# Moving projections, an output projection and the next step's normalisation to other slots of a causal attention stage

## The chip, the cores and the metric

The program runs on one core of a Trainium2 chip. Its engines are TensorE (PE; its weight loads are listed apart as PEld), VectorE (DVE), ScalarE (ACT), GpSimd (POOL) and SyncE (SP), which here issues nearly all transfers. Each engine executes its own instructions in the order of the program and waits on semaphores for the others. The metric is the device time of one execution in microseconds; lower is better.

## The reference

A layer of causal attention with a pre-norm, and then a two-layer block of windowed attention with feed-forward. Only the first is touched here. With `x` of 4 x 1024 x 256 (four batch steps of 1024 tokens), 16 heads of 16 channels:

```python
def _layernorm(x, axis=-1, eps=1e-05): ...
def _L0_attn_ref(x, wq, bq, wk, bk, wv, bv, wo, bo):
    ...
    q = proj(wq, bq); k = proj(wk, bk); v = proj(wv, bv)
    scores = jnp.einsum('bhqd,bhkd->bhqk', q, k) * scale
    mask = jnp.triu(jnp.full((t, t), NEG, jnp.float32), k=1)
    attn = jax.nn.softmax(scores + mask, axis=-1)
    out = jnp.einsum('bhqk,bhkd->bhqd', attn, v)
    ...
    return out @ wo + bo
x = x + _L0_attn_ref(_layernorm(x, axis=-1), ...)
x = x + _L0_ffn_ref(_layernorm(x, axis=-1), ...)
```

All in float32. The normalisation has no gain or bias here; the second one, ahead of the feed-forward layers, is of the same form.

## The kernel before

The causal stage takes about the first 720 us; the two layers behind it take the rest, and nothing of them changes. The instructions of the causal stage stand in an order written out by hand: what is called first stands first on its engine.

**Chunks and slots.** The work is cut into 16 chunks `n` of four heads: chunk `n` belongs to batch step `b = n // 4`, and `c = n % 4` is its place in the step. Each chunk has 12 slots `u` (`NU = 12`). In a slot, `pair` (called twice, for two heads each) puts on PE the transposed scores `t` of chunk `n` (keys on partitions) and the scores `s` of chunk `n+1` (queries on partitions), both line 418. ACT makes the exponentials `et` from `t` (line 442), DVE takes the maxima of `s` (lines 430 and 436), which go into chunk `n+1`'s queries as an extra row so that its exponentials need no subtraction. So chunk `n+1` needs its `qbuf` and `kbuf` one chunk ahead of its own exponentials.

**Masks.** In slots 0 to 3 and 8 to 11 the block of keys crosses the diagonal. There POOL clears the part above the diagonal in `et` (`affine_select`, line 448), once for two heads, before the product with the values may read it. In slots 4 to 7 no mask is needed. The products `av` with the values (line 481) come two slots later (`LAG = 2`). A slot that holds a piece of side work for PE issues these products in one part, another slot in two parts of half the width.

**Banks.** The `t` scores have three PSUM banks, the `s` scores four; the side work's results (`pp`, `pv`, `pr`) use the banks of `s`. One product bank `av` is kept.

**Side work.** After the pairs of a slot come the functions that a plan holds for it (`plan[n][u]`, filled by `put`):

- `norm(b, t0, t1)`: DVE takes mean and variance of token tiles of step `b` (`bn_stats`, `bn_aggr`, lines 264 and 265), POOL the power -0.5 (line 161).
- `prep_x(b, t2)`: POOL normalises two token tiles into `xn` (line 275).
- `turn_x(b, g, i)`: DVE transposes two tiles in 32 x 32 blocks into `xturn` (line 298). Its second call for a group `g` of four tiles (`i = 1`) also issues 16 transfers of 32 KB from SP (line 308), which put the blocks in their places in `xnT`, the transposed, normalised input. There is one `xnT` buffer.
- `project(b, d, which, h)`: 16 matmuls (line 252) of `xnT` with `wq` (`which` = 0) or `wk` (1), for the channels of half `d` and the 256 tokens of quarter `h`; ACT adds the bias and writes the result to `dense` (line 365). There is one `dense` buffer each for q and k, so half `d+1` goes where half `d` was. Quarters 0 and 1 read group 0 of `xnT`, quarters 2 and 3 group 1.
- `spread(n, h)`: eight transfers from SP (line 377), which copy chunk `n`'s heads for 512 tokens out of `dense` into `qbuf` and `kbuf`.
- `put_maxima(n, half)`: DVE turns the maxima, SP sends them to DRAM (`way`, line 462) and, when these have landed, into the queries (line 465).
- `put_out`, `put_oT`: the products are divided by their sums and transposed; SP copies them to `oT` (four transfers, line 513).
- `out_b(b, t2)`: 32 matmuls (line 252, `pr`) with `wo` for two token tiles; ACT copies the result, POOL adds it to `x` (line 534). `out_s` takes the statistics for the next normalisation (DVE, then POOL's power); `out_c` normalises into `y_sb` on POOL (two instructions of line 557).

`quarters(n, b, d, first, *slots)` puts one projection in each of the slots named: q and k alternate, quarters ascend, starting from the place `first`. `outs(n, u, b, t2)` puts `out_b` in slot `u`, `out_s` one slot on, `out_c` three slots on. A slot number of 12 or more counts on into the next chunk.

**Where the touched work stands.** For a step `b`, the first chunk (`c == 0`: chunks 0, 4 and 8, and chunk 12, which has no step behind it) holds projections of half 1 of its own step and the statistics of step `b+1`; the second chunk (1, 5, 9) finishes the transposition of step `b+1` and projects its half 0; the third chunk goes on with that from its slot 0. In chunk 9, as an example, the plan before is: slot 0 `out_b(1,3)`, `spread(11,1)`, `turn_x(3,0,1)`; slot 1 `out_s(1,3)`, `prep_x(3,2)`; slot 2 `prep_x(3,3)`; slot 3 `out_c(1,3)`, `turn_x(3,1,0)`; slot 4 `turn_x(3,1,1)`; projections in slots 5, 6, 8 and 10, and in slot 0 of chunk 10 `project(3,0,0,2)`. `put_oT` of the chunk before stands in slot 3, `put_maxima` of the chunk behind in slots 4 and 11. Chunk 5 has two `scale_tab` on POOL besides (line 118).

Of the kernel before, what the change touches and what calls it, by code (L numbers as in the profile page):

```python
# [50 lines left out]
def kernel_body(  # L51
# [122 lines left out]
    with actx:  # L174
# [68 lines left out]
        NU = 12  # L243
# [322 lines left out]
        def put(n, u, fn, *a):  # L566

            plan[n + u // NU][u % NU].append((fn, a))

        def outs(n, u, b, t2):  # L570
            put(n, u, out_b, b, t2)
            put(n, u + 1, out_s, b, t2)
            put(n, u + 3, out_c, b, t2)

        def quarters(n, b, d, first, *slots):
            for i, u in enumerate(slots):
                put(n, u, project, b, d, (first + i) % 2, (first + i) // 2)

        for n in range(NCH):
            b, c = divmod(n, NC4)  # L580
            more = b + 1 < B
            if n >= 1:
                put(n, 2, put_out, n - 1, 1)
                put(n, 3, put_oT, n - 1, 1)
            if n + 1 < NCH:
                put(n, 4, put_maxima, n + 1, 0)
                put(n, 11, put_maxima, n + 1, 1)
            put(n, 6, put_out, n, 0)
            put(n, 7, put_oT, n, 0)
            if c == 0:  # L590
                if b:
                    quarters(n, b, 1, 3, 0, 2, 4, 6, 8)
                    outs(n, 7, b - 1, 2)
                    outs(n, NU, b - 1, 3)
                    put(n, 1, spread, n + 2, 0)
                    put(n, 3, spread, n + 3, 0)
                else:
                    quarters(n, b, 1, 2, 0, 1, 3, 4, 6, 8)
                    put(n, 2, spread, n + 2, 0)
                    put(n, 3, spread, n + 3, 0)  # L600
                put(n, 9, spread, n + 2, 1)
                put(n, NU, spread, n + 3, 1)
            if c == 0 and more:
                for i, u in enumerate((5, 7, 9, 10)):
                    put(n, u, norm, b + 1, 2 * i, 2 * i + 2)
                put(n, 8, prep_x, b + 1, 0)
                put(n, 10, turn_x, b + 1, 0, 0)
                put(n, 10, prep_x, b + 1, 1)
                n += 1
                put(n, 0, turn_x, b + 1, 0, 1)  # L610
                put(n, 1, prep_x, b + 1, 2)
                put(n, 2, prep_x, b + 1, 3)
                put(n, 3, turn_x, b + 1, 1, 0)
                put(n, 4, turn_x, b + 1, 1, 1)
                quarters(n, b + 1, 0, 0, 5, 6, 8, 10)
                n += 1
                quarters(n, b + 1, 0, 4, 0, 2, 3, 4)
                for i in range(2):
                    put(n, i, spread, n + 2 + i, 0)
                    put(n, 5 + 2 * i, spread, n + 2 + i, 1)  # L620
                for i in range(4):
                    put(n, (6, 8, 10, 13)[i], prep_b, b + 1, i)
                n += 1
                quarters(n, b + 1, 1, 0, 3, 5, 7)
                n -= 3
            if c == 3:
                outs(n, 9, b, 0)
                outs(n, 11, b, 1)
        n = -1
# [737 lines left out]
```

## Time and profile before

| | before |
|---|---|
| median of 3 runs | 1952.52 us (1952.07 to 1953.71) |
| the profiled execution | 1950.3 us |
| its span, first to last instruction | 1948.5 us |
| mean granted clock of PE | 0.973 |
| PE busy | 1883.4 us (97%) |
| DVE busy | 1345.5 us (69%) |
| ACT busy | 1006.4 us (52%) |
| POOL busy | 1029.3 us (53%) |
| `et<-t`, ACT line 442 | 327.8 us |
| `et<-et`, POOL line 448 | 102.5 us in 256 instructions, 407 ns each |

The chain of waits that ended last goes through PE for 86% of the span. A matmul's end is modelled, so a PE that is shown as busy may also be waiting: what a stage costs is read from the distances between its slots, by the first exponential (ACT, line 442) of each slot. The first exponential of a chunk starts at 55.0 us in chunk 0, 94.6 in chunk 1, 229.4 in chunk 4, 270.4 in chunk 5, 407.7 in chunk 8, 448.3 in chunk 9, 496.9 in chunk 10, 658.7 in chunk 14 and 694.1 in chunk 15.

Times in views are microseconds from the span's start. A row of a timeline has the start, the time taken, the engine and line, what is written from what, and how many instructions are merged; a row of a stretch has its length, then each engine's busy time in it, the granted clock and the share of the transfer engines.

### The profile page before, as it was taken

To read this page: it belongs to the slowest core of one execution; us is meant where nothing else is said; L and a number is where in the kernel's file an instruction comes from. 1 tells how busy PE (TensorE), PEld (TensorE's weight loads), DVE (VectorE), ACT (ScalarE), POOL (GpSimd) and SP (SyncE) were. 2 spreads that over 40 slices of the span, in tenths; PEclk is the share of its full clock that TensorE was granted. 3 is DMA by queue.
4 is the path that set the end of the run, shared out by engine and by line. 5 is a ranking of instruction groups with operands and counts; after the bars stand their busy time and mean duration, and the time that the engine had idled before them with its cause. 6 is when DMAs were issued, how large, how long until landed. Compare 5 with 4: busy or idle time off the path is not lost.

```text
span 1948.5 us, 51314 instructions
## 1 busy us (share of the span) xinstructions
PE 1883.4 (97%) x19258; PEld 1026.8 (53%) x19258; DVE 1345.5 (69%) x4092; ACT 1006.4 (52%) x2649; POOL 1029.3 (53%) x1268
## 2 busy tenths in 40 slices
PE   8999999999999978988999999999999999999899
PEld 4333333333333324656566665666666566566575
DVE  6766777677767835676776777786687677678643
ACT  1546555654656653554455555545555554555521
POOL 3222362245224247676765675676676676676621
PEclk8979999998999998999999999999999999999999
DMA  3122111202201011045555555556565655665520
GB/s 116 26 34 76 24 35 32 62 21 38 57 17 29 11 34 68 7 70 98 93 102 92 90 106 101 116 105 111 94 146 108 108 110 101 116 110 101 99 49 22
DMA packets 785127, 142.86 MB, mean 73 GB/s; under 512 B 753536, under 2 KB 775792, under 8 KB 784368
## 3 DMA queue, kind: packets, MB, share of 16 engines
q1 hardware_dynamic: 784624, 139.32, 36.9%
q8 instruction: 153, 2.51, 0.5%
q14 instruction: 94, 0.77, 0.1%
q10 hardware_dynamic: 256, 0.26, 0.1%
HBM read 21.25 MB, written 8.65 MB: 15 GB/s over the span
## 4 chain that ended last, share of the span: by engine, by line
PE 86%; DVE 4%; SPq 3%; POOL 2%; issue 2%; ACT 1%; DMA 1%; ACTq 0%; DVEq 0%; POOLq 0%
PE t L418 15%; PE pag L1155 15%; PE pf L1179 8%; PE av L481 7%; PE pw L1065 6%; PE pq L796 5%; PE pk L796 5%; PE pv L796 5%; PE plo L1023 4%; PE ls L943 3%; PE pp L252 3%; SPq L895 3%; PE pv L252 2%; PE s L418 2%; PE pr L252 1%
## 5 line engine op out<-in xcount | busy, mean ns | idle before, releaser
L442 ACT ACTIVATE et<-t 128x512 f32<-128x512 f32 (+2 forms) x744 | 327.8, 490 | 231.8 <-PE s L418 211.2
L418 PE MATMUL t<-qbuf,kbuf 32*128 32x512 f32 (+2 forms) x1488 | 394.5, 551 | 2.5 <-ACT et L442 2.4
L418 PE MATMUL s<-kbuf,qbuf 16*128 16x512 f32 (+3 forms) x1440 | 382.0, 553 | 2.5 <-DVE mx L436 2.1
L1155 PE MATMUL pag<-hnT,w 128*128 128x512 f32 x704 | 312.1, 592 | 0.8 <-DVE hnT L1139 0.8
L976 ACT ACTIVATE e<-e,lnmx 128x192 f32<-128x192 f32 (+2 forms) x512 | 224.1, 439 | 40.9 <-DVE lnmx L969 40.4
L418 PEld LDWEIGHTS t<-qbuf,kbuf 32*128 32x128 f32 x1488 | 143.4, 188 | 168.8 <-ACT et L442 111.2
L448 POOL TENSOR_SCALAR_AFFINE_SELECT et<-et 128x256 f32<-128x256 f32 x256 | 102.5, 407 | 219.1 <-ACT et L442 218.7
L990 POOL TENSOR_SCALAR e<-e,lrsum 128x192 f32<-128x192 f32 (+2 forms) x512 | 205.7, 423 | 19.4 <-DVE lrsum L987 13.9
L1155 PEld LDWEIGHTS pag<-hnT,w 128*128 128x128 f32 x704 | 131.4, 190 | 142.2 <-issue 134.9
L481 PE MATMUL av<-et,v_sb 128*32 128x256 f32 (+5 forms) x2240 | 186.7, 405 | 6.5 <-POOL et L448 4.7
L436 DVE TENSOR_REDUCE mx<-s 128x1 f32<-128x512 f32 x240 | 153.3, 682 | 57.2 <-PE s L418 55.1
L835 POOL TENSOR_TENSOR rn<-ss,mhalf 128x16 f32<-128x16 f32 x64 | 188.1, 2939 | 5.3
L1179 PE MATMUL pf<-w,act 128*128 128x256 f32 x768 | 173.1, 379 | 0.0
L832 POOL TENSOR_TENSOR rot<-rot,m 128x1024 f32<-128x1024 f32 x64 | 151.2, 2363 | 34.8 <-DVE m L813 29.0
L1179 PEld LDWEIGHTS pf<-w,act 128*128 128x128 f32 x768 | 145.8, 190 | 26.6 <-issue 7.2
L1169 DVE SCALAR_TENSOR_TENSOR act<-pag,cols_sb,ge 128x512 f32<-128x512 f32 x80 | 59.4, 743 | 140.0 <-ACT ge L1168 101.3
L430 DVE CUSTOM_DVE_ANT_0 junk<-s,mask_c 128x512 f32<-128x512 f32 (+3 forms) x240 | 106.8, 485 | 62.4 <-PE s L418 59.8
L418 PEld LDWEIGHTS s<-kbuf,qbuf 16*128 16x128 f32 x1440 | 141.4, 189 | 11.2 <-DVE mx L436 5.2
L430 DVE CUSTOM_DVE_ANT_0 junk<-s,mask_c,mx 128x512 f32<-128x512 f32 (+3 forms) x240 | 121.0, 546 | 37.6 <-PE s L418 36.4
L969 DVE CUSTOM_DVE_ANT_0 e<-ls,mask_h 128x192 f32<-128x192 f32 x408 | 116.8, 351 | 22.5 <-PE ls L943 22.5
L481 PEld LDWEIGHTS av<-et,v_sb 128*32 128x32 f32 x2240 | 45.4, 109 | 164.1 <-issue 115.1
L1065 PE MATMUL pw<-wlo,loT 128*128 128x256 f32 x512 | 127.0, 391 | 1.4 <-issue 0.8
(294 smaller groups left out, 3367.8 us busy)
## 6 DMA issues: line engine op xcount, KB each, us to landing
ring_sb<-turned SPq DMA_DIRECT2D x880, 96.0 KB
qbuf<-dense SPq DMA_DIRECT2D x128, 32.0 KB
oT<-t SPq DMA_DIRECT2D x128, 32.0 KB
x_keep<-x SPq DMA_DIRECT2D x4, 1024.0 KB
xr<-x_keep SPq DMA_DIRECT2D x8, 512.0 KB
out_dram<-y_sb SPq DMA_DIRECT2D x16, 256.0 KB
kbuf<-dense SPq DMA_DIRECT2D x120, 32.0 KB
x<-in_x_dram SPq DMA_DIRECT2D x3, 1024.0 KB
```

Source lines behind the costliest of these rows:

```text
L418: nc.tensor.matmul(o, lhsT=lhsT, rhs=rhs, start=True, stop=True)
L430: nc.vector.tensor_tensor_reduce(out=junk[:, 0:w], in0=ss[h][:, 0:w], in1=mask_c[:, 512 - w : 512], scale=1.0, scalar=mxs[n + 1, i][:, h : ...
L436: nc.vector.tensor_reduce(acc, ss[h][:, 0:w], AX.X, ALU.max)
L442: nc.scalar.activation(et[:, h % 2, c0:512], ts[h][:, c0:512], AF.Exp, scale=ASCALE)
L481: nc.tensor.matmul(av[32 * j : 32 * j + 32, lo:hi], lhsT=v_sb[b % 2][:, kt, VW * (4 * c + j) : VW * (4 * c + j) + STRIP], rhs=ets[j // 2][ ...
L796: nc.tensor.matmul(pq[i], lhsT=lhs[c], rhs=wt[:, c, i * INNER : (i + 1) * INNER], start=(c == 0), stop=(c == 1),)
L835: nc.gpsimd.tensor_tensor(rn[:, :, 0], ss, mhalf, ALU.pow)
L976: nc.scalar.activation(e[:, i, lo:nk], e[:, i, lo:nk], AF.Exp, bias=nmx[:, h : h + 1], scale=-1.0, accum_out=sums[:, h : h + 1],)
L990: nc.gpsimd.tensor_scalar(e[:, i, lo:nk], e[:, i, lo:nk], rsum[:, h : h + 1], 1.0, ALU.mult, ALU.mult)
L1065: nc.tensor.matmul(pw[:, 0:D], lhsT=oT[:, c, :], rhs=wt[:, c, :], start=(c == 0), stop=(c == 3))
L1155: nc.tensor.matmul(pg[half], lhsT=wt[:, c, ff * P : (ff + 1) * P], rhs=hnT[:, c, :], start=(c == 0), stop=(c == 1),)
L1179: nc.tensor.matmul(pf[:, 0:D], lhsT=act[:, f, i * P : (i + 1) * P], rhs=wt[:, f, :], start=(f == 0), stop=(f == NF - 1),)
```

## The change

It alters the plan alone: no instruction's form changes, and no work is added or left out. In short:

- In first chunks with a step behind them, the five (chunk 0: six) projections stand at slots 0, 2, 5, 7, 11 (chunk 0: 0, 2, 4, 7, 9, 11) in place of 0, 2, 4, 6, 8 (0, 1, 3, 4, 6, 8), one side piece for PE to a slot. The output projection of the step before stands at slot 9 in place of 7, and its second one at slot 2 of the second chunk in place of 0, with its `out_s` and `out_c` three and five slots on.
- `spread` of the second halves moves from slot 9 of the first chunk and slot 0 of the second chunk to slots 0 and 1 of the second chunk; in chunk 0 the first halves move one and two slots on as well.
- The next step's `norm` moves from slots 5, 7, 9, 10 to 0, 1, 5, 8; `prep_x` from 8, 10 and then 1, 2 of the second chunk to 4, 7 and then 4, 6; `turn_x` from 10 and then 0, 3, 4 of the second chunk to 9 and then 0, 8, 9.
- The first four projections of the next step stand at slots 4, 6, 8, 10 of the second chunk in place of 5, 6, 8, 10. What follows in the third chunk stays.
- Chunk 12 and everything from there on keeps its plan.

```diff
-        def outs(n, u, b, t2):
+        def outs(n, u, b, t2, wait=1):
             put(n, u, out_b, b, t2)
-            put(n, u + 1, out_s, b, t2)
-            put(n, u + 3, out_c, b, t2)
+            put(n, u + wait, out_s, b, t2)
+            put(n, u + wait + 2, out_c, b, t2)
...
             if c == 0:
-                if b:
+                if b and more:
+                    quarters(n, b, 1, 3, 0, 2, 5, 7, 11)
+                    outs(n, 9, b - 1, 2)
+                    outs(n, NU + 2, b - 1, 3, 3)
+                    put(n, 1, spread, n + 2, 0)
+                    put(n, 3, spread, n + 3, 0)
+                    put(n, NU, spread, n + 2, 1)
+                    put(n, NU + 1, spread, n + 3, 1)
+                elif b:
                     quarters(n, b, 1, 3, 0, 2, 4, 6, 8)
                     outs(n, 7, b - 1, 2)
                     outs(n, NU, b - 1, 3)
                     put(n, 1, spread, n + 2, 0)
                     put(n, 3, spread, n + 3, 0)
+                    put(n, 9, spread, n + 2, 1)
+                    put(n, NU, spread, n + 3, 1)
                 else:
-                    quarters(n, b, 1, 2, 0, 1, 3, 4, 6, 8)
-                    put(n, 2, spread, n + 2, 0)
-                    put(n, 3, spread, n + 3, 0)
-                put(n, 9, spread, n + 2, 1)
-                put(n, NU, spread, n + 3, 1)
+                    quarters(n, b, 1, 2, 0, 2, 4, 7, 9, 11)
+                    put(n, 3, spread, n + 2, 0)
+                    put(n, 5, spread, n + 3, 0)
+                    put(n, NU, spread, n + 2, 1)
+                    put(n, NU + 1, spread, n + 3, 1)
             if c == 0 and more:
-                for i, u in enumerate((5, 7, 9, 10)):
+                for i, u in enumerate((0, 1, 5, 8)):
                     put(n, u, norm, b + 1, 2 * i, 2 * i + 2)
-                put(n, 8, prep_x, b + 1, 0)
-                put(n, 10, turn_x, b + 1, 0, 0)
-                put(n, 10, prep_x, b + 1, 1)
+                put(n, 4, prep_x, b + 1, 0)
+                put(n, 7, prep_x, b + 1, 1)
+                put(n, 9, turn_x, b + 1, 0, 0)
                 n += 1
                 put(n, 0, turn_x, b + 1, 0, 1)
-                put(n, 1, prep_x, b + 1, 2)
-                put(n, 2, prep_x, b + 1, 3)
-                put(n, 3, turn_x, b + 1, 1, 0)
-                put(n, 4, turn_x, b + 1, 1, 1)
-                quarters(n, b + 1, 0, 0, 5, 6, 8, 10)
+                put(n, 4, prep_x, b + 1, 2)
+                put(n, 6, prep_x, b + 1, 3)
+                put(n, 8, turn_x, b + 1, 1, 0)
+                put(n, 9, turn_x, b + 1, 1, 1)
+                quarters(n, b + 1, 0, 0, 4, 6, 8, 10)
```

## The prediction

> **What bounds the kernel now.** I read the page first, then the granted clock, then stretches of the causal stage (0 to about 720 us), and then the queues inside one stretch. S.u below means slot u; a slot starts where ScalarE's timeline shows its first exponential. Chunk 9 (step 2's second chunk of heads) runs from 448.3 to 496.9.
>
> ```profile
> span 1948.5 us, 51314 instructions
> ```
> The profiled execution took 1950.3 us, so 1.8 us lie outside this span; the median of the three runs is 2.2 us more (1952.5).
>
> ```profile
> 658.70:694.10 35.40, 34.84 (x372) 13.52 (x374) 28.74 (x88) 21.86 (x50) 7.65 (x18) 1.00 0.12 40
> 94.60:148.10 53.50, 53.37 (x462) 18.93 (x462) 34.52 (x110) 26.38 (x60) 16.14 (x28) 0.74 0.19 32
> 270.40:326.00 55.60, 51.45 (x486) 18.00 (x486) 35.37 (x115) 27.17 (x61) 26.19 (x36) 0.88 0.18 31
> 448.30:500.70 52.40, 51.12 (x486) 18.47 (x486) 35.28 (x115) 27.19 (x61) 21.68 (x34) 0.87 0.19 33
> 448.50:455.30 6.80, 6.80 (x38) 2.12 (x42) 3.65 (x16) 2.10 (x4) 4.64 (x8) 0.50 0.07 15
> 469.00:475.80 6.80, 6.71 (x38) 2.31 (x38) 5.05 (x11) 2.37 (x5) 1.84 (x2) 0.50 0.28 49
> 407.70:411.40 3.70, 3.70 (x48) 1.38 (x44) 3.33 (x11) 2.63 (x6) 2.23 (x4) 1.00 0.09 21
> 411.40:413.80 2.40, 2.32 (x32) 1.07 (x24) 2.33 (x12) 2.17 (x5) 2.40 (x3) 1.00 0.25 55
> ```
> These are stretches: length, busy time of PE, PEld, DVE, ACT and POOL, granted clock, DMA share, GB/s. A chunk without side work takes 35.4 us (first row). The next three start with chunks 1, 5 and 9 and reach to the end of slot 0 of the chunk behind: 53.5, 55.6 and 52.4 us, with five projections each (and, in the second and third, an output projection), at a clock below 1. The clock is lost in pieces such as the fifth and sixth rows. So the stage has something to win exactly where the diff works.
>
> ```profile
> 461.56 2.43 POOL L275 TENSOR_SCALAR xn<-x,mv,rs_a 128x256 f32<-128x256 f32 x2
> 464.71 2.42 POOL L275 TENSOR_SCALAR xn<-x,mv,rs_a 128x256 f32<-128x256 f32 x2
> 468.42 2.42 POOL L557 TENSOR_SCALAR y_sb<-x,mvo,rs_o 128x256 f32<-128x256 f32 x2
> ```
> POOL's timeline shows why: a normalisation (L275) or an `out_c` (L557) holds POOL for 2.4 us, the exponentials' masks (L448) stand behind it, and the products that need them behind these. PE starves and its clock halves.
>
> **What the change removes.** `prep_x` goes from masked slots (S.8, S.10, S.1, S.2) to S.4, S.7, S.4, S.6, `out_c` from S.3 to S.7: in the second chunk POOL no longer stands in front of masks. What that is worth is seen from where PE reaches the first projection of the next step, `project(b+1,0,0,0)`. Now:
>
> ```profile
> 474.29 1.81 PE L252 MATMUL pp<-xnT,wq_sb 128*32 128x256 f32 x16
> 498.65 1.07 PE L252 MATMUL pp<-xnT,wq_sb 128*32 128x256 f32 x16
> ```
> The first row is that projection, 26.0 us after chunk 9's start; the second is `project(b+1,0,0,2)`, the first that reads the other half of the tokens, in slot 0 of chunk 10. Without POOL's stalls PE would come to the end of S.4 after slots of 3.07, 2.43, 4.07 (2.5 and an output projection, 1.57 by slot 0 with and without one in chunks 13 and 14), 2.89 and 1.9 (S.4's 3.93 less the 2.0 from a projection's start to the next slot): 14.4 us. Chunk 1 has no output projection there: 12.8.
>
> **What it adds: two waits for SP.** `project` reads `xnT`, which `turn_x` fills with 16 transfers, and all of a group's 16 must have landed. SP issues them one after another.
>
> ```profile
> 453.25 2.42 SPq L377 DMA_DIRECT2D qbuf<-dense  x4
> 455.71 2.49 SPq L377 DMA_DIRECT2D kbuf<-dense  x4
> 458.32 11.20 SPq L308 DMA_DIRECT2D xnT<-xturn  x16
> 469.65 2.45 SPq L513 DMA_DIRECT2D oT<-t  x4
> 472.20 11.53 SPq L308 DMA_DIRECT2D xnT<-xturn  x16
> 496.30 1.70 SPq L462 DMA_DIRECT2D way<-mt  x4
> 499.05 0.55 SPq L465 DMA_DIRECT2D qbuf<-way  x1
> ```
> A `spread` is 5.07 us of SP (453.25 to 458.32), a `turn_x` group 10.5 to 11.8 over its six occurrences (mean 11.3). Traffic of the second group fades about 1.5 us after its last issue (DMA share 0.29, then 0.04 from 485.0 on, issue over at 483.73).
>
> First wait. In the second chunk SP has: the five transfers of `put_maxima` (done 2.7 after the chunk's start where nothing is late, by 499.05+0.55 against 496.9), `spread(n+2,1)`, which the change puts in front here (5.07), then the 16, which it does not shorten. 2.8+5.1+11.3+1.5 = 20.6. PE is there at 14.4 (12.8 in chunk 1), since the projection goes from S.5 to S.4: a wait of 6.2 to 7.8 us. Behind it on PE stand S.5's scores, so ACT's exponentials and DVE's maxima wait too. Before, the transfers had landed at about 471.0 and PE came at 474.3: nobody saw them.
>
> `spread(n+3,1)` now stands behind these 16 as well; its four q copies land about 20.6+2.4 = 23.0 after the start, and ACT's write of the single `dense` buffer must wait for that. The projection ends at 21.7 to 22.4, so ACT is late by up to 1.3; PE has S.5's first half to do (1.07 to 2.0), which covers it: 0, and 1.3 without that cover. `put_oT` and `put_maxima` behind them slip to about 30; their readers come in S.0 of the next chunk, at 45 or later: 0.
>
> Second wait. The second `turn_x` goes from S.4 to S.9, its reader stays in slot 0 two slots later.
>
> ```profile
> 491.24 0.09 DVE L430 DVE_READ_ACCUMULATOR2_ANT nmax<- 128x1 f32 x1
> ```
> DVE's S.9 ends here, at S.10's start (491.4). Two transposes (0.75, and some 0.3 from the pair newly in S.8) end 1.0 after it; 11.3 of issue and 1.5 to land make 13.8. PE's natural arrival is 498.65-491.4 = 7.3: a wait of 6.5 us. Before, the group was issued by 483.73, 13 us ahead of need.
>
> Both waits idle PE for longer than the starvation that halves the clock now: in the fifth row above, PE resumed its products at 450.62 and ran at 0.50 until 455.3, 4.7 us that cost half, 2.3 us. I charge 2.3 for each wait; bounds 0 and 3.4 (all 6.8 us of such a row).
> The Trainium skill ("TensorE: Matmul & The Clock Gate", section "Why this matters for your kernels") warns of PE-idle gaps above about 3 us, one idle window putting the clock back to half; the rows here agree (0.50 for 6.8 us), and the rule speaks against the change as soon as either wait binds.
> The skill's "DMA: Bandwidth & Descriptors" (section "Anatomy of one DMA") gives about 2.0 us of fixed cost for a transfer on another path; by that, in place of the 1.5 seen, each wait would be 0.5 longer and the sum 3 us higher.
>
> **The sum, second chunk to end of slot 0 behind it.** To the first projection 20.6; from there 2.0 to S.5, then S.5 to S.9 at chunk 9's and 10's lengths 3.17+4.07+3.43+3.93+2.69 = 17.3, the transposes 0.3, clock 2.3: 21.9; then 13.8 to the second projection; 2.0 and clock 2.3 behind it: 4.3. Together 60.6. Against 53.5, 55.6 and 52.4: +7.1, +5.0, +8.2 = +20.3. In chunk 5 two `scale_tab` still delay masks; that is hidden under the first wait, 0.
>
> First chunks (0, 4, 8): the same projections at other slots, at the same PE price (a piece costs its slot 0.6 to 0.9 wherever it stands). What moves is DVE: a `norm` call is 1.5 us of it (442.95 to 444.48). S.0 and S.1 held 3.33+2.33 = 5.7 of DVE in 6.1 us (last two stretches); two calls make 8.7, and with a half slot (1.2) that DVE may lag before its PSUM banks run out, +1.4. S.8 +0.6; S.11 loses its jam (3.3 against 2.4): -0.9. I take +1.1 each, +3.3; bounds -1 and +2.5 each.
>
> Sum: +23.6 on 1950.3 is 1973.9, and at the distance of the median 1976.
>
> **Rivals.** (a) Only one wait binds. If the second group were there in time, the stretch would lose 6.5+2.3 and come to 51.8, against 53.8 on average: 3 x -2.0, and +3.3 for the first chunks: 1950, no change. For it: the wait is one estimate of issue; against: 16 issues never took under 10.4 us in this stage, and only 7.3 are there.
> (b) Faster: neither binds. The place is SP's order in the second chunk; the price is both waits and clocks, about 9 us each, and it decides if a group lands within 12.8 us of the chunk's start and 7.3 us of S.10. Then 42.8 a stretch: 3 x -11.0 + 3.3, 1923. For it: POOL's stalls are real and go. Against: `spread` and 16 issues alone are 16.4 us.
> (c) Worse: the clock stays low, as from 97.0 to 124.3 in chunk 1, where 27.3 us ran at 0.50. Half of that less the 4.6 already charged is 9 more at most, and nothing at least, as chunk 1's stretch was no longer than the others; 5 a batch give 1991. Against: four of the five low pieces there lasted 6.8 us.
> (d) The waits bind but the clock costs nothing and DVE absorbs the norms: 1976-13.8-3.3 = 1959.
>
> **Numbers.** Forecast with its spread of clock cost 0.75; (a) 0.05; (b) 0.05; (c) 0.08; (d) 0.07. The time is the forecast's, 1976. The range goes from a little below (d), as SP's price may be 1 us smaller a wait, to (c): 1957 to 1991. Within 0.2% (3.9 us) is about what a measurement here can't tell from no change. Faster by more: 0.07; same: 0.05; slower: 0.88.
>
> **What would show it.** In the changed profile: POOL's L275 rows between S.4 and S.7, no PE idling at the second chunk's start; PE's row of L252 in S.4 ended by the DMA of `xnT`, about 20.6 after the chunk's start; PE idle before slot 0's projection by about 6 us, with `xnT<-xturn` x16 on SP just ahead; half clock at both places; chunks 0, 4 and 8 about 1 us longer. It is wrong if either L252 row follows its products without a pause, or if the chunks of the second kind end under 49 us.

## Result: both waits came as forecast, and the half clock behind them lasted twice as long

The changed kernel takes 1995.06 us (median of 4 runs, 1992.24 to 2002.06) against 1952.3 us for the one before it (4 runs, 1950.0 to 1953.71): a ratio of 1.0228, 95% interval 1.020 to 1.0255. It is slower, as forecast, but by 42.8 us where the forecast had 23.6, and its time lies above the range that was given. The profiled execution took 1992.24 us, 41.9 more than the profiled one of before.

From the page of the changed kernel, its span, the busy times of the engines and the shares of the chain that ended last:

```profile
span 1990.5 us, 51297 instructions
...
PE 1890.3 (95%) x19250; PEld 1031.4 (52%) x19250; DVE 1345.7 (68%) x4092; ACT 1005.7 (51%) x2649; POOL 1029.9 (52%) x1268
...
PE 85%; SPq 5%; DVE 4%; issue 2%; POOL 2%; DMA 1%; ACT 1%; ACTq 0%; DVEq 0%; POOLq 0%
```

Every engine works as long as before to within 7 us, so nothing was added; the mean clock fell from 0.973 to 0.963. SP's queue has 5% of the chain, against 3% before; new in it are the issues of line 308, with 3%.

The stretches that the forecast is made for, from the start of chunks 1, 5 and 9 to the end of slot 0 of the chunk behind (length, busy time of PE, PEld, DVE, ACT and POOL, granted clock, share of the transfer engines, GB/s), and below them the pieces right behind the two waits in chunk 9 and 10:

```profile
95.70:158.80 63.10, 48.35 (x456) 17.26 (x453) 33.07 (x103) 26.26 (x60) 13.28 (x24) 0.82 0.18 31
285.10:346.80 61.70, 49.46 (x488) 17.73 (x480) 34.33 (x108) 26.74 (x61) 24.50 (x32) 0.84 0.18 32
473.30:534.90 61.60, 49.49 (x488) 17.82 (x480) 34.31 (x108) 26.71 (x61) 19.98 (x30) 0.84 0.18 33
491.00:504.60 13.60, 11.81 (x68) 3.76 (x72) 5.04 (x11) 4.21 (x8) 2.74 (x3) 0.50 0.17 36
528.60:542.20 13.60, 10.93 (x80) 4.07 (x84) 3.36 (x15) 3.83 (x10) 1.22 (x3) 0.50 0.19 38
```

The first three took 53.5, 55.6 and 52.4 us before and were forecast at 60.6. The last two rows carry the surprise: behind each wait the clock is at 0.50 for 13.6 us, not 6.8, with PE busy for all but 2 to 3 us of it.

PE's timeline at the two waits (start, time taken, instructions; in brackets the idle time ahead and what ended it):

```profile
116.47 1.93 PE L252 MATMUL pp<-xnT,wq_sb 128*32 128x256 f32 x16 [7.94 <-DMA xnT<-xturn]
155.15 1.94 PE L252 MATMUL pp<-xnT,wq_sb 128*32 128x256 f32 x16 [6.25 <-DMA xnT<-xturn]
305.71 1.94 PE L252 MATMUL pp<-xnT,wq_sb 128*32 128x256 f32 x16 [6.50 <-DMA xnT<-xturn]
492.79 1.94 PE L252 MATMUL pp<-xnT,wq_sb 128*32 128x256 f32 x16 [5.38 <-DMA xnT<-xturn]
```

Both kinds of projection wait for the transfers into `xnT`: the first, third and fourth rows are `project(b+1,0,0,0)` in slot 4, the second is `project(b+1,0,0,2)` in slot 0 of the third chunk. SP's queue over chunk 9 shows why they land late (start, time that the issues took, transfers):

```profile
474.87 0.53 SPq L465 DMA_DIRECT2D qbuf<-way  x1
475.50 2.43 SPq L377 DMA_DIRECT2D qbuf<-dense  x4
477.97 2.48 SPq L377 DMA_DIRECT2D kbuf<-dense  x4
480.56 10.84 SPq L308 DMA_DIRECT2D xnT<-xturn  x16
491.44 2.50 SPq L377 DMA_DIRECT2D qbuf<-dense  x4
...
518.11 11.50 SPq L308 DMA_DIRECT2D xnT<-xturn  x16
```

The first 16 begin when SP has issued the spread that now stands ahead of them, and their last issue is over at 491.40, 1.4 us before PE starts. The second 16 are issued by 529.61; PE, ready for them at about 524.8, starts at 531.3.

POOL's long instructions have moved. In the old chunk 9 its two normalisations and an `out_c` ran at 461.6 to 470.9. Now one normalisation falls on the first wait, and the other, like `out_c(1,3)`, on slots without masks. Only `out_c(1,2)`, which moves from slot 10 of chunk 8 to slot 0 of chunk 9, stands in front of two masks; it costs nothing, as slots 0 and 1 take 3.14 and 2.43 us in chunk 9 and in chunk 1, which has no `out_c`. These are the rows of `out_c(1,2)` and of the first normalisation:

```profile
476.31 2.43 POOL L557 TENSOR_SCALAR y_sb<-x,mvo,rs_o 128x256 f32<-128x256 f32 x2
...
485.87 2.42 POOL L275 TENSOR_SCALAR xn<-x,mv,rs_a 128x256 f32<-128x256 f32 x2
```

Masks were not the only way by which POOL held PE up in the old chunk 9. DVE's transpose for `put_oT` sat idle there until POOL had divided the products (line 501), which stood behind the two normalisations. The maxima stood behind that transpose, and PE's next scores behind the maxima:

```profile
467.75 0.71 DVE L510 STREAM_TRANSPOSE t<-t 128x512 f32<-128x512 f32 x1 [2.85 <-POOL t L501]
```
```profile
469.09 1.22 PE L418 MATMUL s<-kbuf,qbuf 16*128 16x512 f32 x1 [0.68 <-DVE mx L436]
```

Ahead of the old chunk 9, from 440.0 to 448.3, the chain that ended last runs through DVE, with the `norm` calls of slots 9 and 10. The change moves these too. So what it relieves there is POOL's and DVE's work together, and no run separates the two.

By chunks (start of one chunk's first exponential to the next one's), in us. The untouched chunks 3, 7, 11 and 12 to 15 are the same in both to 0.1 us:

| chunks | before | after | difference |
|---|---|---|---|
| 0, 4, 8 | 39.6, 41.0, 40.7 | 39.0, 41.9, 41.9 | +1.5 |
| 1, 5, 9 | 49.8, 51.9, 48.6 | 51.4, 50.8, 49.7 | +1.6 |
| 2, 6, 10 | 42.3, 42.6, 42.3 | 53.3, 52.7, 53.2 | +32.0 |
| ahead of chunk 0 | 55.0 | 56.7 | +1.7 |
| last causal exponential to the end | 1230.8 | 1235.8 | +5.0 |

These add up to the 41.9 of the two profiles, but for rounding. In chunks 1, 5 and 9 the wait for SP costs slightly more than the relief gives; in chunks 2, 6 and 10 there was nothing to relieve, and the second wait is a plain loss of some 10.7 us each. The last two lines are code that no edit touches.

### The profile page after: what moved, and what is told of

The parts are those of the page before. It is cut to its first block, busy times and chain, and to the rows that moved or that the text cites. A ratio compares the mean times of both kernels' runs of the same rounds, so it can differ in the third digit from the quotient of the medians.

```text
span 1990.5 us, 51297 instructions
## 1 busy us (share of the span) xinstructions
PE 1890.3 (95%) x19250; PEld 1031.4 (52%) x19250; DVE 1345.7 (68%) x4092; ACT 1005.7 (51%) x2649; POOL 1029.9 (52%) x1268
## 4 chain that ended last, share of the span: by engine, by line
PE 85%; SPq 5%; DVE 4%; issue 2%; POOL 2%; DMA 1%; ACT 1%; ACTq 0%; DVEq 0%; POOLq 0%
PE t L418 15%; PE pag L1165 14%; PE pf L1189 8%; PE av L481 7%; PE pw L1075 6%; PE pq L806 5%; PE pk L806 5%; PE pv L806 5%; PE plo L1033 4%; PE ls L953 3%; PE pp L252 3%; SPq L308 3%; SPq L905 2%; PE pv L252 2%; PE pr L252 1%
## 5 line engine op out<-in xcount | busy, mean ns | idle before, releaser
L986 ACT ACTIVATE e<-e,lnmx 128x192 f32<-128x192 f32 (+2 forms) x512 | 224.1, 439 | 41.5 <-DVE lnmx L979 41.0
```

Source lines behind the costliest of these rows:

```text
L986: nc.scalar.activation(e[:, i, lo:nk], e[:, i, lo:nk], AF.Exp, bias=nmx[:, h : h + 1], scale=-1.0, accum_out=sums[:, h : h + 1],)
```

## The experiments

Each is an edit of the changed kernel unless it says otherwise. Ratios are to the kernel before the change, run beside each on the same chip (its medians were 1949.6 to 1953.3). The plan has two cases for the first chunk, so an edit of `c == 0` was made in both; the diffs show the one for later steps.

### The second wait alone: transposition earlier

```diff
-                put(n, 6, prep_x, b + 1, 3)
-                put(n, 8, turn_x, b + 1, 1, 0)
-                put(n, 9, turn_x, b + 1, 1, 1)
+                put(n, 5, prep_x, b + 1, 3)
+                put(n, 5, turn_x, b + 1, 1, 0)
+                put(n, 6, turn_x, b + 1, 1, 1)
```

> The changed kernel with the second group of transfers earlier: in the second chunk prep_x of the last two tiles goes from slot 6 to 5, the second turn_x from slots 8 and 9 to 5 and 6. All else as changed. Theory (two waits for SP, each with a spell of half clock behind it): the second wait goes. In the changed trace slot 0 of chunks 2, 6 and 10 takes 11.6, 10.9 and 11.9 us against 3.7, and slots 1 and 2 behind it about 3 us more than at full clock: 11.0 + 10.1 + 10.9 = 32 us, so 1995 - 32 = 1963. Slot 0 of those chunks about 3.7, slot 4 of chunks 1, 5, 9 still 11 to 14. Rival (the loss is in the new places of the side pieces and norms, DVE late): 1995, as none of these moves.

Measured: 1964.93 us, ratio 1.0063 (1.0040 to 1.0086). Slot 0 of chunks 2, 6 and 10 is back at 3.71 us each and these chunks are at 42.3, 42.6 and 42.3, exactly as before the change; slot 4 of chunks 1, 5 and 9 still lasts 13.4, 12.5 and 11.8. So the second wait is made by the place of that `turn_x` on SP, and it costs the 32 us of the table: 10.7 a wait, of which 6.1 is PE's mean idle time (6.25, 5.5, 6.5). The other 4.6 go with the half clock; the filled version below tests that.

### The first wait alone, and both

The first wait was avoided by letting its reader come later:

```diff
-                quarters(n, b + 1, 0, 0, 4, 6, 8, 10)
+                quarters(n, b + 1, 0, 0, 7, 8, 9, 10)
```

> The changed kernel with the four projections of the next step at slots 7, 8, 9, 10 of the second chunk in place of 4, 6, 8, 10: they come after the first group of transfers has landed, about 20 us into the chunk. Theory: the first wait and its half clock go. Slots 4, 5 and 6 of chunks 1, 5 and 9 took 13.6, 11.7 and 10.7 us more than at full clock without the wait: 36 us, so 1995 - 36 = 1959; slot 0 of chunks 2, 6, 10 still 11 to 12. Rival (side pieces in neighbouring slots cost as much as the wait, because DVE and the PSUM banks limit slots 7 to 9): 1985 to 1995.

Measured: 1970.45 us, ratio 1.0089 (1.0058 to 1.0120); 24.6 us of the 36 expected. Slot 4 fell to 3.35 as foreseen, but slot 8 of chunks 1, 5 and 9 rose from 3.9 to 7.86, 4.04 and 6.65, and slot 9 from 2.69 to 4.78, 3.82 and 5.89.

Then with the edit of the first experiment as well:

> The two edits together: transfers of the second group earlier, projections of the next step at slots 7 to 10. Theory: no wait for SP is left, and what remains is the gain from POOL's order: 1995 - 32 - 36 = 1927, faster than the kernel before (1952) by about 25; clock near 1.00 through chunks 1, 5 and 9, each about 40 us long. Rival (POOL's order is worth nothing, the kernel before lost its time there to side pieces and DVE): about 1952.

Measured: 1942.16 us, ratio 0.9942 (0.9924 to 0.9960): faster than before the change, but 15 us more than expected. Chunks 1, 5 and 9 take 42.7, 41.1 and 41.5 against 49.8, 51.9 and 48.6 before the change, so the relief is real: 25 us over the three. Of the 15 us that were missed, some 9 lie in these chunks, more than half of it in slot 8 (7.99, 4.09 and 5.29 for 3.9), and 3.7 in the later layers, which no edit touches. DVE's timeline in chunk 1 of this kernel, and SP's queue ahead of it, show what slot 8 waits for:

```profile
122.87 0.71 DVE L510 STREAM_TRANSPOSE t<-t 128x512 f32<-128x512 f32 x1 [4.00 <-DMA oT<-t]
```
```profile
115.61 3.21 SPq L377 DMA_DIRECT2D kbuf<-dense  x4
118.93 2.43 SPq L513 DMA_DIRECT2D oT<-t  x4
```

`put_oT`'s four transfers read the one buffer that DVE's next transpose writes. They stand in SP's order behind the spreads and the 16, leave at 118.93 to 121.36, and DVE waits 4.00 us for them to land, with its maxima behind it and PE's banks behind those. In the changed kernel the same transfers go out just as late, but there PE itself is late and nobody notices. A wait that is removed uncovers the next one on the same queue.

### The price of the clock alone

24 products of an identity matrix, ahead of each of the two projections that wait. They go into one of the four PSUM banks of the `s` scores, nothing reads them, and they are to keep PE from idling while both waits stay:

```diff
+            if b and d == 0 and which == 0 and h % 2 == 0:
+                fill = one(f"fill_{b}_{h}")
+                for _ in range(24):
+                    nc.tensor.matmul(fill[:, 0:P], lhsT=ident, rhs=ident, start=True, stop=True)
```

> The changed kernel with 24 matmuls of the identity with itself ahead of each of the two waiting projections, into a spare bank that nobody reads: PE waits as long, but isn't idle. It measures the clock's share apart from the waits'. Theory (the waits are as forecast, 5.4 to 7.9 us of idle PE, and the half clock behind each costs 4.4 to 5.7 us and not 2.3): the six spells of half clock go, 30 us, so 1965, with slots 5 and 6 of chunks 1, 5, 9 and slots 1 and 2 of chunks 2, 6, 10 back at their lengths before. Rival (the clock costs the 2.3 us each that were charged, and the waits are longer than forecast): 1981. Rival (the matmuls come on top): over 2010.

Measured: 1975.04 us, ratio 1.0117 (1.0085 to 1.0150). The low clock in the causal stage went from 85.3 to 13.7 us in the profile, and the stage from 698.0 to 679.7 us. Where it returned to full, the slots say what it had cost: in chunk 1, slots 4 to 6 went from 13.82, 5.19, 5.82 to 12.09, 3.17, 4.08, 5.5 us less; in chunk 2, slots 0 to 2 from 11.64, 3.81, 5.09 to 9.55, 2.43, 3.39, 5.2 less; in chunks 6 and 10 the same three slots took 3.2 and 4.5 less. Chunks 5 and 9 gained nothing; a spell of 6.8 us is left in each. In chunk 5 PE runs ahead of the wait's end and pauses in another place:

```profile
292.29 5.62 PE L356 MATMUL fill<-ident 128*128 128x128 f32 x48 [0.62 <-DVE mx L440]
...
298.37 1.07 PE L252 MATMUL pp<-xnT,wq_sb 128*32 128x256 f32 x16 [0.45 <-DMA xnT<-xturn]
```
```profile
296.88 2.50 SPq L381 DMA_DIRECT2D qbuf<-dense  x4
```
```profile
301.92 0.47 ACT L369 ACTIVATE dense<-pp,cols_sb 128x256 f32<-128x256 f32 x1 [9.35 <-PE s L422]
```

The projection takes 1.07 us, not 1.94, and ends at 299.44; ACT's write of `dense` starts only at 301.92, 2.5 us after the last of the spread's q copies was issued (299.38). The trace names an earlier releaser for the 9.35, so that the write waits for these copies to leave the single `dense` buffer is inferred from the plan and the times. It comes 1.4 to 2.5 us after the projection's end in the three chunks. The time lies between the 1965 expected and the 1981 of the rival, 10 us from the one and 6 from the other. What is shown: of the changed kernel's loss at least 18.3 us is clock and not waiting, since both waits for the transfers are still there. What the two spells left over would give is not shown.

### Shortening the first wait: one spread earlier

```diff
-                    quarters(n, b, 1, 3, 0, 2, 5, 7, 11)
+                    quarters(n, b, 1, 3, 0, 2, 5, 7, 8)
...
-                    put(n, NU, spread, n + 2, 1)
+                    put(n, 9, spread, n + 2, 1)
```

> The changed kernel with the first chunk's projections at slots 0, 2, 5, 7, 8 (chunk 0: 0, 2, 4, 6, 7, 8), as early as before the change, so that spread of the second half (eight transfers, 5.07 us of SP) stands at slot 9 again, as before the change, and not ahead of the 16 transfers in the second chunk. The projections that wait stay at slots 4 and 0. Theory (the first wait is SP's order: 2.7 + 5.1 + 11 + 1.5): the first wait shrinks by 5.1, from 7.9, 6.5 and 5.4 us of idle PE to 2.8, 1.4 and 0.3 in chunks 1, 5 and 9; xnT's 16 transfers begin about 2.8 after the chunk's start in place of 7.3 to 7.8. With the half clock behind it gone as well: 36 - 5 = 31 us less, 1964; if so short a wait still halves the clock: 1980. Slot 0 of chunks 2, 6, 10 stays at 11 to 12. Rival (DVE's transposes or the landing hold the group, not the issue ahead of it): 1995.

Measured: 1974.23 us, ratio 1.0114 (1.0082 to 1.0146). SP's queue in chunk 9 of this kernel, and PE's timeline at the waits of chunks 1 and 9:

```profile
464.22 0.53 SPq L465 DMA_DIRECT2D qbuf<-way  x1
464.86 11.44 SPq L308 DMA_DIRECT2D xnT<-xturn  x16
```
```profile
109.31 1.33 PE L252 MATMUL pp<-xnT,wq_sb 128*32 128x256 f32 x16 [3.74 <-DMA xnT<-xturn]
...
477.70 1.08 PE L252 MATMUL pp<-xnT,wq_sb 128*32 128x256 f32 x16 [3.15 <-DMA xnT<-xturn]
```

The 16 now follow `put_maxima` directly, and PE's idle time fell from 7.94, 6.50 and 5.38 us to 3.74, 2.45 and 3.15. The clock was still halved behind each, for 10.2, 6.8 and 10.2 us, and slots 5 and 6 stay near 5.2 each. So the shorter wait keeps most of the clock's price: the time is 10 us over the 1964 expected and 6 under the 1980 named for a clock that still halves.

### Two ways to put them together

The version with both waits avoided, and `spread(n+3,1)` three slots later so that `put_oT` goes ahead of it:

```diff
-                    put(n, NU + 1, spread, n + 3, 1)
+                    put(n, NU + 4, spread, n + 3, 1)
```

> The kernel with both edits (second group early, projections at 7 to 10), and spread(n+3,1) at slot 4 of the second chunk in place of 1, so that SP issues put_oT's four transfers ahead of it. In the kernel with both edits slot 8 of chunks 1 and 9 took 8.0 and 5.3 us against 3.9: DVE's transpose for put_oT (L510) sat idle from 118.87 to 122.87 in chunk 1, until SP's four transfers from its single buffer t3, issued from 118.93 on, had landed. Theory (a third queue on SP: the transfers of oT stand behind both groups): slot 8 back to 3.9 to 4.1 in all three, 5 us less than 1942, 1937. Rival (slot 8 is long because side pieces stand in every slot from 7 to 10): 1942, slot 8 as long.

Measured: 1947.88 us, ratio 0.9982 (0.9962 to 1.0002): no gain, a miss. Slot 8 is mended (3.64, 4.09, 4.09), but with PE sooner, the second group is late again in chunks 2 and 10. SP's queue in chunk 1 and PE's wait in slot 0 of chunk 2:

```profile
101.13 11.61 SPq L308 DMA_DIRECT2D xnT<-xturn  x16
112.84 2.46 SPq L513 DMA_DIRECT2D oT<-t  x4
...
125.21 11.37 SPq L308 DMA_DIRECT2D xnT<-xturn  x16
```
```profile
138.31 1.94 PE L252 MATMUL pp<-xnT,wq_sb 128*32 128x256 f32 x16 [2.95 <-DMA xnT<-xturn]
```

An idle time of 2.95 us is enough: 13.65 us of half clock follow, the projection takes 1.94, and slot 0 lasts 8.33 against 3.71.

The other way takes one spread out of the second chunk (the edit above for it), transposes the second group early, and projects in slots 5, 6, 8 and 10:

> spread early as in the first of this call, the second group of transfers early (prep_x at 4 and 5, turn_x at 5 and 6), and the next step's projections at slots 5, 6, 8, 10 as before the change. PE comes to slot 5's projection about 17.6 us after the chunk's start, the first group lands at 2.8 + 11.3 + 1.5 = 15.6, dense is free at 18.1, and put_oT's transfers are issued by about 21.7. Theory: no wait is left, chunks 1, 5 and 9 take 40 to 41 us and the whole 1935 to 1940, with POOL's order of the change. Rival (something else than SP's order and transfers holds these chunks): over 1950.

Measured: 1922.76 us, ratio 0.9845 (0.9819 to 0.9871), better than expected and faster than both kernels. Its stretches:

```profile
96.30:139.40 43.10, 41.67 (x457) 16.02 (x456) 33.25 (x103) 26.17 (x60) 13.29 (x24) 1.00 0.23 39
262.00:306.80 44.80, 44.55 (x492) 16.73 (x488) 34.11 (x109) 26.83 (x60) 24.80 (x33) 1.00 0.22 38
431.10:474.90 43.80, 43.55 (x492) 16.43 (x488) 34.28 (x109) 26.55 (x60) 20.26 (x31) 1.00 0.23 39
```

The same counts of work on PE as in the changed kernel, to a few records, in 43 to 45 us instead of 61.6 to 63.1, at full clock. This is about what rival (b) put at 42.8.

One step further, with the projections at 6, 7, 8 and 10:

> The fastest so far (spread early, second group early, projections at 5, 6, 8, 10) with the projections at 6, 7, 8, 10. In its trace slot 5 of chunks 1, 5 and 9 took 5.5, 5.5 and 4.5 us against 3.9: a last wait for SP at slot 5. Theory: at slot 6 no wait is left, and two projections in slots 6 and 7, which DVE bounds anyhow, cost less than in others: 1.0 to 1.6 us less in each of the three, 1919 against 1922.8. Rival (what e6 showed, that PE then comes sooner to the second group): slot 0 of chunks 2, 6, 10 longer than 3.7 and 1923 or more.

Measured: 1925.67 us, ratio 0.9869 (0.9846 to 0.9892), beside the 0.9845 above: no better. Chunks 1, 5 and 9 became shorter by 1.4, 0.2 and 0.2 us, chunks 4 and 8, which the step does not touch, longer by 2.8 and 1.5: each has 6.83 us of half clock in slot 2, where the version before it has 3.41 in chunk 8 alone.

### Two queues for the 16 transfers

```diff
-                    nc.sync.dma_start(
+                    (nc.scalar if a % 2 else nc.sync).dma_start(
```

> The changed kernel with every second of turn_x's 16 transfers issued from ACT in place of SP (both groups); plan as changed. Theory (SP's issue, one after another, is what makes both waits, not the transfer of the bytes): a group takes about 5.5 us in place of 11, and all six waits shrink by 5 to 5.5: from 7.9, 6.5, 5.4 and 6.3, 5.5, 6.5 to about 2.5, 1, 0 and 1, 0, 1. If waits that short still halve the clock, as the 2.4 to 3.7 us in the kernel with spread early did, 6 x 5.3 = 32 us less, 1963; without it 1935 to 1940. ACT's own issue (8 x 0.6 us a group) may hold exponentials back by up to 5 us a group, 1995 at most. Rival (the transfer engines are the limit): waits as long, 1995 or more.

Measured: 1998.00 us, ratio 1.0254 (1.0218 to 1.0290): a miss. The time is that of the rival (1995 or more), but not for its reason. SP's queue and ACT's timeline at the first group of chunk 9:

```profile
478.13 5.24 SPq L308 DMA_DIRECT2D xnT<-xturn  x8
```
```profile
474.29 6.76 ACTq L308 DMA_DIRECT2D xnT<-xturn  x8
481.15 1.25 ACT L442 ACTIVATE et<-t 128x384 f32<-128x384 f32 x3 [7.79 <-DMA xnT<-xturn]
```

Eight issues take SP 5.24 us, half of 16, and the last is over 12.5 us after the chunk's start, against 18.1 in the changed kernel. Slot 4 is down to 4.00, though PE comes to it later as well. So the late landing was one queue's issue and not the bytes. But ACT's eight take 6.76 us of ACT, with the exponentials queued behind them idle for 7.79. Slot 0 of chunks 1, 5 and 9 rises from 3.14 to 10.3 to 10.8, slot 9 from 2.69 to 8.6 to 8.9. The wait moved to an engine that PE depends on.

### The layers behind, which no edit touches

> The kernel before, unchanged, for a second trace. The two layers behind the causal stage, which nothing touches, took 1230.8 us in its first trace (from the last exponential of the causal stage to the end) and 1235.8 to 1240.2 in the traces of the changed kernel and the first four. If that is a draw of each execution: a value elsewhere in 1231 to 1240 here. If the change or the later start lengthens them: 1231 again.

Measured: 1952.23 us in one run. From the last causal exponential to the end, the profiles show 1230.8 and 1233.3 us for the unchanged kernel, 1235.8 for the changed one, and 1229.0 to 1240.2 for the nine edited ones. So 5.0 of the 41.9 us lie in code that is the same, within what one profile differs from another by; what sets it was not found. The same holds for the 1.7 us ahead of chunk 0: that start, which no edit touches, took 54.3 to 59.8 us in the twelve profiles.

## Why the prediction was right in kind and short in size

**Where PE would wait, and how long: right.** The first projection was to come 20.6 us after the chunk's start; it came at 20.8, 20.6 and 19.5. PE was to idle for 6.2 to 7.8 there; it idled 7.94, 6.50 and 5.38. (The terms as printed make 20.7; with 2.7 and 5.07 in place of 2.8 and 5.1 they make 20.6.) From slot 10 to the second projection 13.8 was worked out; chunks 1, 5 and 9 had 13.6, 12.8 and 13.8, with 6.25, 5.5 and 6.5 of idle time against 6.5. Adding up what stands on SP between the transposes and the landing was enough for that, and the first and second experiments each removed the wait that they aimed at. The reading that POOL no longer stands in front of masks in the second chunk overlooked the one `out_c` that moves there; it cost nothing. And POOL's way to PE was in part through DVE, as the rows above show.

**The first chunks: smaller than forecast.** +3.3 was charged for DVE's work that moves there; it was +1.5, inside the bounds. By slots it was not as worked out. The two `norm` calls cost slots 0 and 1 nothing and show in slot 2 of chunks 4 and 8, 4.57 for 3.40 with DVE busy for 4.49 of it in chunk 4; slot 11 did not lose 0.9 but rose from 3.33 to 3.70, with a projection there now.

**The waits put at nothing.** ACT's write of `dense` came 0.5, 2.1 and 0.9 us after the first projection's end, where up to 1.3 was worked out and given as hidden; the way from there to slot 10 was no longer in chunk 5, which had the 2.1, than in the others. `put_oT`'s slip was hidden too, since PE was late for another reason; the version with both waits avoided shows it as 4.00 us of DVE. Neither is part of the miss.

**The step that failed: "I charge 2.3 for each wait; bounds 0 and 3.4 (all 6.8 us of such a row)."** This term was mis-sized. From the first projection to slot 10 the forecast had 19.6 us and 2.3 for the clock; measured were 25.1, 24.6 and 24.7, so about 5.2. Behind the second projection, slot 0's rest took 3.6 where 2.0 was natural. Slots 1 and 2 of the third chunk, which the sum had as unchanged, took 3.81 and 4.76 to 5.09 for 2.43 and 3.40. Together 1.6 + 2.9 = 4.5. The row used as a price had 6.8 us of half clock, with PE shown as busy throughout and no idle time of more than 1 us ahead of it. Behind these waits six spells of half clock follow, five of 13.6 to 13.7 us and one of 17.1, and PE's work is 11 to 13 us of each. The miss is then (2.9 + 2.2) x 3 = 15 us, and the filled version, which took the idle time away, confirms the size where the clock came back to full: 5.5, 5.2, 3.2 and 4.5, 4.6 on average.

**The rest.** The forecast's 23.6, with 15 for the clock, -1.8 for the first chunks, 1.7 ahead of chunk 0 and 5.0 in the later layers, is 43.5 against the 41.9 of the profiles; the 1.6 between them are waits that were a little shorter than worked out.

**The rivals.** (c), a clock that stays low, priced at 5 a batch, was the nearest at 1991. It was set against four low pieces of 6.8 us in the profile before; ahead of those PE was idle for at most 2.2 us in one piece, not for 5 to 8. The fifth piece, of 27.3 us, was a sign that a spell can be longer. (b) is what the change would have been without SP: the two versions with the waits avoided or shortened gained 0.6% and 1.5%, and the second came at 1922.76 where (b) had 1923. The Trainium skill's rule on idle gaps ("TensorE: Matmul & The Clock Gate", "Why this matters for your kernels") pointed the right way: all six gaps, of 5.4 to 7.9 us, had half clock behind them. Its 3 us are no threshold in these traces, where gaps of 2.3 to 3 us had half clock behind them too. Nor did the rows of before show the rule, as the prediction had it: they show the half clock, but no such gap.

## What to carry to other kernels

When a step is moved, add up the seconds of every transfer that its queue issues between the producer and the reader, with those that change places with it; here that gave both waits to within 1.1 us. Price an idle PE as the wait plus the half clock behind it, and take the second from a row behind a whole idle gap, with wide bounds; work a few slots past the wait pays for it too, so the sum has to reach there. Where one queue issues nearly all transfers, shortening one wait shows the next on the same queue, and giving half of the issues to an engine that computes blocks its computing: look instead for the transfers that can leave earlier, as one spread could here.

## What the runs showed of the hardware

- In the causal stage of all these traces the half clock comes in whole pieces of 3.41 us, and their number does not follow the idle time in front of it. In the changed kernel gaps of 5.4 to 7.9 us had four pieces behind them (13.65 us), once five. In the edited kernels gaps of 4.8 to 7.5 us had two to seven, and gaps of 2.9 to 3.7 three or four. Gaps of 2.27, of 1.78 and of 2.45 with one of 1.45 behind it had two, one of 2.62 had one, and one of 1.79 none. The gap of 8.5 us at the stage's end, in code that is the same in all, had two or three.
- Some spells had no gap of PE over 1 us ahead of them, as the profile shows it: 27.3 us in chunk 1 before the change, 6.83 in slot 2 of chunks 4 and 8 of the version with projections at 6, 7, 8 and 10. So the 5 us are the price of these six gaps and not of any gap, and what sets the number of pieces was not found.
- A transfer of 32 KB in this form keeps its issuing queue for about 0.7 us, on SP (10.84 and 11.50 us for 16) and a little more on ACT (6.76 us for 8), while the transfer engines stand at a share of 0.17 to 0.19.
- Code that is the same to the last instruction, some 1230 us of it, differed by 11 us between profiles of kernels with other work ahead of it. The cause is open.
